# Layer 0 of a four-layer convolution network: the statistics of image 0 on partitions of (channel, half of the image)

## The chip, the cores and the metric

The kernel runs on one core of a Trainium2 chip. The metric is the device time in microseconds of one execution; lower is better. A core has a matrix engine (TensorE, PE in the profile), a vector engine (VectorE, DVE), an activation engine (ScalarE, ACT), GpSimd (POOL), a sync engine (SyncE, SP) that in this kernel issues the loads, and 16 DMA engines that move data between HBM and the on-chip memory. That memory has 128 partitions.

## The reference

The input `x` has 4 images of 64 channels of 256 x 256, in float32. Four layers follow one another, each a residual around a convolution of a group norm:

```python
def _gn(v, G=32, eps=1e-5):
    B_, C_, H_, W_ = v.shape
    g = v.reshape(B_, G, C_ // G, H_, W_)
    m = jnp.mean(g, axis=(2, 3, 4), keepdims=True)
    s = jnp.var(g, axis=(2, 3, 4), keepdims=True)
    return ((g - m) / jnp.sqrt(s + eps)).reshape(v.shape)

x = x + _L0_conv_ref(_gn(x), w_in, w_dw, fft_filter, w_out)
x = x + _L1_conv_ref(_gn(x), kernel)
x = x + _L2_conv_ref(_gn(x), core, periphery, threshold, scale, 1, 1)
x = x + _L3_conv_ref(_gn(x), weights1, weights2)
```

The group norm takes mean and variance of 2 neighbouring channels over the whole image, so nothing of layer 0 can be normalized for an image before all of that image has been read once. Layer 0 then expands 64 channels to 384, multiplies 8 x 8 patches by a filter in the frequency domain, applies a 3 x 3 depthwise convolution, gates one half of the channels by the gelu of the other, and projects back to 64. Layer 1 is a 3 x 3 convolution, layer 2 a choice between two convolutions by a local difference measure, layer 3 a multiplication of low Fourier modes.

## The kernel before, in words

The four layers run one after the other, each from HBM to HBM. Layer 0 has two phases.

*The statistics of image 0* (L256 to L263) come first and alone. A loop over NJ = 32 steps allocates a tile `st` of 128 partitions x 4 rows x 256 columns out of 12 buffers and fills it with two loads (L261), which SyncE issues: channels of one band of four rows into partitions 0 to 63, channels of the next band into partitions 64 to 127. So a partition is (band of the pair, channel), each load moves 64 rows of 4 KB, and within a load the rows are a whole channel, 256 KiB, apart. VectorE runs two `bn_stats` of 512 columns on each tile (L253, in `input_stats`), which leave count, mean and squared deviation of each piece per partition.

`group_norm_parts` (L153 to L175) makes scale and bias of them: `bn_aggr` to mean and variance per partition (`mv`, L158), a TensorE product with the 128 x 128 matrix `avg` that averages the means over a group of partitions (L161), a copy of the result (`gm`, L163), the deviation of each partition from it (`d`, L165) and its square plus the variance (`q`, L167), a second product with `avg` (L170), then the power -0.5 on GpSimd (`r`, L174) and `nb` = -mean · r on VectorE (L175). `avg` joins the partitions of the same group, which are (half, channel) in everything that comes after: `r` and `nb` are read by `normalize` as scale and bias of partitions (half of the columns, channel).

After that SyncE loads the constants of the layer (`c_fdft` to `woutc`, L138, L279, L283 and L286), into memory that the `st` buffers held, and then the first tiles of `x` (L306). ScalarE normalizes a tile (L210), TensorE transposes and transforms it (L346, L356), and the main loop begins: 128 steps, each with one tile of 8 rows through all parts of the layer. In the loop the order of instructions on TensorE, VectorE, ScalarE and SyncE is the order in which they are written. The statistics of the other images are taken inside this loop, one tile a step (`load_stats`, L568, and `next_stats`), while TensorE is busy; they have the old partition layout and are not touched by the change.

Of the statistics phase, the order is set by the queues: SyncE issues the loads in order and waits with each until the load eight before it has landed, and from the thirteenth tile on until `bn_stats` has freed the buffer; VectorE waits for the load of its tile.

Of the kernel before, what the change touches and what calls it, by code (L numbers as in the profile page):

```python
# [17 lines left out]
C = 64  # L18
# [3 lines left out]
GROUPS = 32  # L22
# [4 lines left out]
def _patch_dft():  # L27


    p = PATCH  # L30
    h, w = np.meshgrid(np.arange(p), np.arange(p), indexing="ij")
    rows, pick = [], []
    for kw in range(p // 2 + 1):
        edge = kw in (0, p // 2)
        for kh in range(p // 2 + 1 if edge else p):
            ang = 2 * np.pi * (kh * h + kw * w) / p
            sel = np.zeros((p, p // 2 + 1))
            sel[kh, kw] += 0.5 if edge else 1.0
            if edge:
                sel[(-kh) % p, kw] += 0.5  # L40
            rows.append(np.cos(ang).ravel())
            pick.append(sel.ravel())
            if not (edge and kh in (0, p // 2)):
                rows.append(np.sin(ang).ravel())
                pick.append(sel.ravel())
    fwd = np.array(rows)
    inv = np.linalg.inv(fwd)
    pick = np.array(pick)
    twice = lambda m: np.concatenate([m, m], 0)
    return twice(fwd.T), twice(inv.T), twice(pick).T  # L50


def _fno_dft(H, W):
    m = MODES
    kh = np.concatenate([np.arange(m), np.arange(-m, 0)])
    kw = np.arange(m)
    ah = 2 * np.pi * np.outer(np.arange(H), kh) / H
    eh = np.stack([np.cos(ah), -np.sin(ah)], -1).reshape(128, H // 128, 4 * m)
    aw = 2 * np.pi * np.outer(np.arange(W), kw) / W
    cw, sw = np.cos(aw), np.sin(aw)  # L60
    ew = np.stack([np.concatenate([cw, -sw], 1), np.concatenate([sw, cw], 1)], 1)
    ew = ew.reshape(W // 128, 128, 2, 2 * m)
    ei = np.stack([np.cos(ah), -np.sin(ah)], 0).transpose(2, 0, 1)
    ei = ei.reshape(2, m, 2, H).transpose(2, 1, 0, 3).reshape(2 * m, 2, H)
    ck = np.where(kw == 0, 1.0, 2.0)[:, None] / (H * W)
    iw = np.concatenate([ck * cw.T, -ck * sw.T], 0)
    return eh, ew, ei, np.concatenate([iw] * 4, 0)


def _constants(H, W):  # L70
    f_blk, b_blk, pick = _patch_dft()
    eh, ew, ei, iw = _fno_dft(H, W)
    grp = (np.arange(128) % C) // (C // GROUPS)
    avg = (grp[:, None] == grp[None, :]) / np.sum(grp == 0)
    half = np.arange(128) // C
    ones = half[:, None] == half[None, :]


    g32 = (np.arange(128) % 32) // (C // GROUPS)
    avg32 = (g32[:, None] == g32[None, :]) / np.sum(g32 == 0)  # L80
    chan = np.arange(128) % C
    sel32 = np.stack([np.arange(128)[:, None] + 32 * k == chan[None, :] for k in range(2)], 1)
    sel32[32:] = False
    out = {
        "c_ident": np.eye(128), "c_avg32": avg32, "c_sel32": sel32, "c_fdft": f_blk, "c_bdft": b_blk, "c_pick": pick, "c_avg": avg,
        "c_ones": ones, "c_eh": eh, "c_ew": ew, "c_ei": ei, "c_iw": iw,
    }
    return {k: np.ascontiguousarray(v, dtype=np.float32) for k, v in out.items()}
# [26 lines left out]
class _Net:  # L115
# [34 lines left out]
        for _ in self.group_norm_parts(*args):  # L150
            pass

    def group_norm_parts(self, n, b, bst, psum):  # L153


        nc, sp = self.nc, self.sp
        mv = sp.tile([128, 2], F32, tag="mv", name=f"mv{n}_{b}")
        nc.vector.bn_aggr(mv, bst.rearrange("p n s -> p (n s)"))  # L158
        yield
        ps = psum(f"gn{n}_{b}")  # L160
        nc.tensor.matmul(ps[:, 0:1], self.avg, mv[:, 0:1], start=True, stop=True)  # L161
        gm = sp.tile([128, 1], F32, tag="gm", name=f"gm{n}_{b}")
        nc.vector.tensor_copy(gm, ps[:, 0:1])  # L163
        d = sp.tile([128, 1], F32, tag="gd", name=f"gd{n}_{b}")
        nc.vector.tensor_sub(d, mv[:, 0:1], gm)  # L165
        q = sp.tile([128, 1], F32, tag="gq", name=f"gq{n}_{b}")
        nc.vector.scalar_tensor_tensor(q, d, d, mv[:, 1:2], ALU.mult, ALU.add)  # L167
        yield
        ps2 = psum(f"gv{n}_{b}")
        nc.tensor.matmul(ps2[:, 0:1], self.avg, q, start=True, stop=True)  # L170
        v = sp.tile([128, 1], F32, tag="gv", name=f"gvs{n}_{b}")
        nc.vector.tensor_scalar(v, ps2[:, 0:1], EPS, None, ALU.add)
        r, nb = self.r[n][:, b : b + 1], self.nb[n][:, b : b + 1]
        nc.gpsimd.tensor_tensor(r, v, self.mhalf, ALU.pow)  # L174
        nc.vector.scalar_tensor_tensor(nb, gm, -1.0, r, ALU.mult, ALU.mult)  # L175
# [53 lines left out]
    def _layer0(self, ctx, dst):  # L229
        tc, nc, a, B, H, W = self.tc, self.nc, self.a, self.B, self.H, self.W  # L230
# [4 lines left out]
        def pair(name):  # L235

            return pp.tile([128, 2, 512], F32, tag=f"p{next(turn) % 4}", name=name)

        small = lambda name: pair(name)[:, 0, :]
# [4 lines left out]
        halves = [slice(0, C), slice(C, 128)]  # L244
        quarters = [slice(k * Q, (k + 1) * Q) for k in range(4)]

        src_t = a["x"].rearrange("b c (j s r) w -> b c j s r w", r=4, s=2)

        def input_stats(t, k, bst):
            tf = t.rearrange("p r w -> p (r w)")  # L250
            n = 4 * W // 512
            for i in range(n):
                nc.vector.bn_stats(bst[:, k * n + i, :], tf[:, i * 512 : (i + 1) * 512])  # L253

        new_bst0 = lambda b: self.stats_tile(f"bst0_{b}", NJ * 4 * W // 512)
        with tc.tile_pool(name="l0i", bufs=12) as p_i:  # L256
            bst0 = new_bst0(0)
            for k in range(NJ):
                t = p_i.tile([128, 4, W], F32, tag="st", name=f"st_{k}")
                for s in range(2):  # L260
                    nc.sync.dma_start(t[halves[s]], src_t[0, :, k, s])  # L261
                input_stats(t, k, bst0)
            self.group_norm(0, 0, bst0, small)  # L263

        cp = pool("l0c", 1)
        p_st, p_x, p_r, p_xn = pool("l0st", 2), pool("l0x", 2), pool("l0r", 2), pool("l0xn", 1)
# [3 lines left out]
        pick, filt = self.load("c_pick", cp), self.load("filt", cp)  # L270
        wdw = self.load("w_dw", cp)
        ps = small("psf")
# [1095 lines left out]
```

## Time and profile before

The time before is 7649.04 us, the median of 3 runs from 7638.49 to 7653.11. The profiled execution has a span of 7652.4 us.

| engine | busy us | share of the span |
|---|---|---|
| PE, matmul | 7291.6 | 95% |
| PE, weight load | 4324.6 | 57% |
| DVE | 6594.1 | 86% |
| ACT | 3656.9 | 48% |
| POOL | 637.7 | 8% |

The busy shares are averages over the whole span. The table by stretches is of more use for a change in one place; the first five stretches, of 20 us each, show how the kernel begins. The last column is what the DMA engines moved.

| stretch, us | PE busy | DVE busy | ACT busy | GB/s |
|---|---|---|---|---|
| 0 to 20 | 0.00 | 8.17 | 0.00 | 211 |
| 20 to 40 | 0.00 | 11.79 | 0.00 | 239 |
| 40 to 60 | 0.00 | 11.40 | 0.00 | 239 |
| 60 to 80 | 1.84 | 12.73 | 0.00 | 176 |
| 80 to 100 | 6.83 | 3.37 | 6.53 | 88 |

The first load of `st` is issued at 1.67 us, the last at 66.0 us; a load takes between 3.4 and 9.2 us from its issue to its landing, 8.7 us in the middle. The last `bn_stats` ends at 75.48 us. ScalarE runs its first normalize at 88.47 us.

### The profile page before, as it was taken

The numbers are of one execution on the slowest core, as the hardware profiler recorded it, in microseconds if no ns is written. First come the engines' busy times: TensorE is split into PE (matmuls) and PEld (weight loads), VectorE is DVE, ScalarE is ACT, GpSimd is POOL, SyncE is SP. The second block draws the span as 40 slices with busy tenths as digits, with TensorE's granted clock in tenths as the row PEclk, the third lists the DMA queues.
The fourth block names the chain that finished last, engine by engine and source line by source line (L and its number), as shares of the span: only waits on it lengthen the run. The fifth ranks groups of instructions, "written<-read, shape, count | busy, mean of one in ns | idle before, by whom it ended". The sixth has DMA issues, their size and how long they took to land.

```text
span 7652.4 us, 398676 instructions
## 1 busy us (share of the span) xinstructions
PE 7291.6 (95%) x189302; PEld 4324.6 (57%) x189302; DVE 6594.1 (86%) x5914; ACT 3656.9 (48%) x3917; POOL 637.7 (8%) x1403
## 2 busy tenths in 40 slices
PE   5999999999999999999999999899989999997887
PEld 3666666666666666666666666433334444443375
DVE  6999999999999999999999999899979989884345
ACT  2445444445454444544444454322238787773111
POOL 0000000000000000000000000010102222221000
PEclk9999999999999999999999999999999999999955
DMA  5222222222222222222111211477766666666689
GB/s 119 62 66 63 59 62 60 59 62 60 64 59 59 60 62 60 65 59 53 45 47 47 49 47 44 113 196 196 198 150 178 176 172 179 172 175 236 226 325 390
DMA packets 502418, 875.49 MB, mean 114 GB/s; under 512 B 42948, under 2 KB 306068, under 8 KB 483380
## 3 DMA queue, kind: packets, MB, share of 16 engines
q1 hardware_dynamic: 420276, 581.48, 27.7%
q0 software_dynamic: 80512, 268.50, 12.2%
q8 instruction: 1485, 24.33, 1.4%
q14 instruction: 145, 1.19, 0.0%
HBM read 581.37 MB, written 268.44 MB: 111 GB/s over the span
## 4 chain that ended last, share of the span: by engine, by line
PE 88%; DVE 4%; DMA 4%; issue 2%; ACT 1%; SPq 0%; DVEq 0%; ACTq 0%; POOLq 0%; POOL 0%
PE psd L434 31%; PE psy L407 10%; PE m L786 9%; PE psu L369 9%; PE one L1038 7%; PE div L997 5%; PE pso L509 3%; DMA x<-x 3%; DVE v L472 2%; PE psz L1027 2%; PE psa L1212 2%; PE psF L356 2%; PE psT L346 2%; PE m L794 1%; PE pso L500 1%
## 5 line engine op out<-in xcount | busy, mean ns | idle before, releaser
L434 PE MATMUL psd<-y,diag 32*32 32x512 f32 x73296 | 2536.7, 597 | 7.5 <-issue 6.1
L472 DVE SCALAR_TENSOR_TENSOR v<-y,sb_w_dw,v 128x2048 f32<-128x2048 f32 x1024 | 2390.8, 2335 | 109.8 <-ACT v L470 87.1
L434 PEld LDWEIGHTS psd<-y,diag 32*32 32x32 f32 x73296 | 1526.1, 103 | 852.5 <-issue 333.8
L414 ACT COPY y<-psy 128x512 f32<-128x512 f32 x1536 | 915.6, 660 | 1691.0 <-PE psy L407 1689.0
L372 DVE TENSOR_TENSOR up<-psu,flt 128x768 f32<-128x768 f32 x1024 | 932.6, 951 | 223.4 <-PE psu L369 222.5
L407 PEld LDWEIGHTS psy<-sb_c_bdft,up 64*64 64x64 f32 x49152 | 858.4, 135 | 345.3 <-issue 132.2
L407 PE MATMUL psy<-sb_c_bdft,up 64*64 64x64 f32 x49152 | 930.2, 221 | 27.5 <-issue 24.6
L369 PE MATMUL psu<-win,xf 64*64 64x384 f32 x8192 | 788.2, 487 | 19.8 <-DVE h L454 10.0
L983 DVE TENSOR_TENSOR q<-xn 128x2313 f32<-128x2313 f32 (+2 forms) x256 | 627.3, 2494 | 10.4 <-ACT xn L210 10.4
L1038 PE MATMUL one<-z,wp 32*32 32x512 f32 x16384 | 591.5, 596 | 17.1 <-issue 14.0
L984 ACT ACTIVATE q<-q 128x2313 f32<-128x2313 f32 (+2 forms) x256 | 529.0, 2086 | 31.2 <-DVE q L983 29.7
L210 ACT ACTIVATE xn<-x,nb,r 128x1024 f32<-128x1024 f32 (+3 forms) x272 | 488.1, 1798 | 57.7 <-DMA x<-x 54.0
L448 ACT ACTIVATE h<-psd 128x1024 f32<-128x1024 f32 x258 | 251.0, 1023 | 516.9 <-PE psd L434 516.7
L1038 PEld LDWEIGHTS one<-z,wp 32*32 32x32 f32 x16384 | 369.9, 103 | 219.8 <-issue 77.9
L997 PE MATMUL div<-q,ones 64*32 64x512 f32 x8192 | 465.1, 596 | 10.3 <-ACT q L984 9.3
L369 PEld LDWEIGHTS psu<-win,xf 64*64 64x64 f32 x8192 | 306.1, 134 | 185.1 <-issue 84.9
L379 POOL MEMSET y<- 128x22 f32 x384 | 51.7, 136 | 4238.0 <-ACT y L387 3175.2
L1071 POOL DMA_DIRECT2D x<-r x512 | 272.8, 540 | 977.2 <-DVE r L1068 949.4
L786 PE MATMUL m<-t,wg 64*64 64x512 f32 x3072 | 343.4, 591 | 11.0 <-DVE t L779 11.0
L786 PE MATMUL m<-t,wk 64*64 64x512 f32 x3072 | 352.7, 588 | 0.0
L997 PEld LDWEIGHTS div<-q,ones 64*32 64x32 f32 x8192 | 153.0, 107 | 314.9 <-issue 243.4
L801 ACT COPY s<-m 128x1024 f32<-128x1024 f32 x64 | 64.8, 1013 | 542.5 <-PE m L786 542.5
(131 smaller groups left out, 7616.3 us busy)
## 6 DMA issues: line engine op xcount, KB each, us to landing
x<-x SPq DMA_DIRECT2D x240, 640.0 KB, 5.7
x<-x SPq DMA_DIRECT2D x61, 2048.0 KB, 12.6
st<-in_x_dram SPq DMA_DIRECT2D x256, 256.0 KB, 3.6
x<-in_x_dram SPq DMA_DIRECT2D x256, 256.0 KB, 3.8
x<-o POOLq DMA_DIRECT2D x128, 512.0 KB, 8.5
r<-x SPq DMA_DIRECT2D x512, 128.0 KB, 4.0
x<-r POOLq DMA_DIRECT2D x512, 128.0 KB, 3.9
out_dram<-x POOLq DMA_DIRECT2D x32, 2048.0 KB, 13.3
```

Source lines behind the costliest of these rows:

```text
L210: self.nc.scalar.activation(dst, src, AF.Identity, bias=self.nb[n][p0:p1, b : b + 1], scale=self.r[n][p0:p1, b : b + 1])
L369: nc.tensor.matmul(ps[halves[n], s, 0:384], xf[t][halves[s], n, 4 * g + k], win[halves[s]], start=True, stop=True)
L372: nc.vector.tensor_mul(ups[t, g][:, :, k, :], ps[:, :, 0:384], flt.broadcast_to([128, 2, 384]))
L407: nc.tensor.matmul(ps[halves[c], n, s, :, k, :], up[halves[n], s, k, i * 128 + c * C : i * 128 + (c + 1) * C], bdft[halves[n]], start=True ...
L414: nc.scalar.copy(yt[t][i][:, 3:11, w0 : w0 + 64].rearrange("p r (k n w) -> p n r k w", k=4, n=2), ps[:, :, s])
L434: ins = nc.tensor.matmul(d[q // 2][quarters[j], q % 2], diag[quarters[q], i, k, :], rows_in(t, i, quarters[q], j, dy)[:, :, dx : dx + W], ...
L472: nc.vector.scalar_tensor_tensor(v, s, wdw[:, 2, k : k + 1], v, ALU.mult, ALU.add)
L786: nc.tensor.matmul(rows2(m)[halves[j], s], gs[i][halves[s], dx, :], ts[n][halves[s], i, 2 * j : 2 * j + 2, dx : dx + W], start=(dx == 0), ...
L983: nc.vector.tensor_sub(d, p0, p1)
L984: nc.scalar.activation(d, d, AF.Square)
L997: ins = nc.tensor.matmul(ps[quarters[j], h], ones[halves[h]], q[n, g, k][halves[h], r + 2 * j : r + 2 * j + 2, o : o + W], start=(m == 0), ...
L1038: ins = nc.tensor.matmul(rows2(ps[g])[quarters[j], k], w[quarters[i]], z[quarters[i], h, 2 * j + dy : 2 * j + dy + 2, dx : dx + W], tile_p ...
```

## The change

The statistics of image 0 are taken on partitions of (channel, half of the image): partition 2c + s holds the rows of half s of channel c. In HBM that is a plain view of the image as 128 rows, each 128 KiB after the one before, so one load fills all 128 partitions of a `st` tile, and the 64 loads of 256 KB become 32 of 512 KB. The tile, its 12 buffers and the two `bn_stats` on it stay.

The group norm then finds its per-partition numbers in another layout than its results are needed in. Two more constant matrices serve that. `c_avgp` averages groups within the new layout and gives each partition the mean that its deviation is measured from. `c_avgx` averages groups of the new layout and writes the result in the old one, (half, channel), so that `r` and `nb` come out where `normalize` reads them. It is used for the mean a second time (one more matmul, and one more copy, into the same tile `gm`) and for the second product. Both matrices are loaded from a pool of their own, `l0a`, ahead of the `st` tiles. The group norms of the other images and layers pass no such pair and run as before.

```diff
+    grpp = np.arange(128) // 2 // (C // GROUPS)
+    avgp = (grpp[:, None] == grpp[None, :]) / np.sum(grp == 0)
+    avgx = (grpp[:, None] == grp[None, :]) / np.sum(grp == 0)
...
-    def group_norm_parts(self, n, b, bst, psum):
+    def group_norm_parts(self, n, b, bst, psum, avg=None):
+        same, moved = avg or (self.avg, self.avg)
...
-        nc.tensor.matmul(ps[:, 0:1], self.avg, mv[:, 0:1], start=True, stop=True)
+        nc.tensor.matmul(ps[:, 0:1], same, mv[:, 0:1], start=True, stop=True)
+        if moved is not same:
+            nc.tensor.matmul(ps[:, 1:2], moved, mv[:, 0:1], start=True, stop=True)
         gm = sp.tile([128, 1], F32, tag="gm", name=f"gm{n}_{b}")
         nc.vector.tensor_copy(gm, ps[:, 0:1])
...
         nc.vector.scalar_tensor_tensor(q, d, d, mv[:, 1:2], ALU.mult, ALU.add)
+        if moved is not same:
+            nc.vector.tensor_copy(gm, ps[:, 1:2])
         yield
         ps2 = psum(f"gv{n}_{b}")
-        nc.tensor.matmul(ps2[:, 0:1], self.avg, q, start=True, stop=True)
+        nc.tensor.matmul(ps2[:, 0:1], moved, q, start=True, stop=True)
...
-        with tc.tile_pool(name="l0i", bufs=12) as p_i:
+        with tc.tile_pool(name="l0i", bufs=12) as p_i, tc.tile_pool(name="l0a", bufs=1) as p_a:
             bst0 = new_bst0(0)
+            flat = a["x"][0].rearrange("c (s h) w -> (c s) (h w)", s=2)
+            avgs = [self.load(name, p_a) for name in ("c_avgp", "c_avgx")]
             for k in range(NJ):
                 t = p_i.tile([128, 4, W], F32, tag="st", name=f"st_{k}")
-                for s in range(2):
-                    nc.sync.dma_start(t[halves[s]], src_t[0, :, k, s])
+                nc.sync.dma_start(t.rearrange("p r w -> p (r w)"), flat[:, 4 * W * k : 4 * W * (k + 1)])
                 input_stats(t, k, bst0)
-            self.group_norm(0, 0, bst0, small)
+            self.group_norm(0, 0, bst0, small, avgs)
```

More of the change, by code (lines that the diff above doesn't have):

```diff
@@ L84, in _constants @@
     out = {
-        "c_ident": np.eye(128), "c_avg32": avg32, "c_sel32": sel32, "c_fdft": f_blk, "c_bdft": b_blk, "c_pick": pick, "c_avg": avg,
+        "c_ident": np.eye(128), "c_avg32": avg32, "c_sel32": sel32, "c_fdft": f_blk, "c_bdft": b_blk, "c_pick": pick, "c_avg": avg, "c_avgp": avgp, "c_avgx": avgx,
         "c_ones": ones, "c_eh": eh, "c_ew": ew, "c_ei": ei, "c_iw": iw,
```

## The prediction

> **What bounds the kernel now.** I read the page first: TensorE is busy 95% of 7652.4 us and the chain that ended last lies 88% on it, so for most of the span a DMA change would buy nothing. The page's slices also show TensorE at 5 tenths in the first slice, and that is where the change is. So the second view is the chain of waits from 0 to 100 us, whose columns are start, length and what the time was spent on:
>
> ```profile
> 6.11 6.81 DMA st<-in_x_dram
> 12.94 8.77 DMA st<-in_x_dram
> ...
> 65.98 8.11 DMA st<-in_x_dram
> 74.19 1.30 DVE bst L253 x2
> ...
> 82.60 4.52 DMA x<-in_x_dram
> 87.18 1.28 ACT L210
> 88.47 1.25 ACT xn L210
> ```
>
> From 6 to 74 us nothing but the loads of `st` is on the path. Then come the last two bn_stats, constants, and loads of `x`; the first normalize starts at 88.47. Third, the timeline of VectorE at the two ends of this stage, and the group of instructions of L253 in the first 110 us (count, busy us, mean ns, idle before them):
>
> ```profile
> 6.44 1.29 DVE L253 BATCH_NORM_STATS2 bst<-st 128x6 f32<-128x512 f32 x2 [5.57 <-DMA st<-in_x_dram]
> ...
> 74.19 1.29 DVE L253 BATCH_NORM_STATS2 bst<-st 128x6 f32<-128x512 f32 x2 [0.46 <-DMA st<-in_x_dram]
> ```
>
> ```profile
> L253 DVE BATCH_NORM_STATS2 bst<-st 128x6 f32<-128x512 f32 x64 | 41.2, 685 | 33.4 <-DMA st<-in_x_dram 33.4
> ```
>
> Each tile has 1.29 us of statistics and then a wait. 31 tile periods fill 74.19 - 6.44 = 67.75 us, 2.185 us each; 524,288 bytes in 2.185 us are 240 GB/s. Fourth, the engines by stretch; the last two numbers of each line are the DMA engines' busy share and GB/s:
>
> ```profile
> 10.00:30.00 20.00, 0.00 (x0) 0.00 (x0) 11.57 (x18) 0.00 (x0) 0.00 (x0) 1.00 1.04 238
> ...
> 7400.00:7500.00 100.00, 82.88 (x463) 63.50 (x463) 59.09 (x95) 12.41 (x21) 8.18 (x10) 0.59 1.04 408
> ```
>
> ```profile
> 7279.00:7282.00 3.00, 3.00 (x62) 3.00 (x61) 0.00 (x0) 0.00 (x0) 0.00 (x0) 0.50 1.02 437
> ```
>
> All three have the DMA engines fully busy, at very different rates. 238 GB/s is the 64-partition `st` loads; 408 is layer 3, with loads and stores on 128 partitions; 437 is a pure load of `wt` on 128 partitions. So the first stage is bound by slow transfers, not by too few of them or by their issue.
>
> **What the Trainium skill says.** First, "SBUF — State Buffer", section "Door 1: The DMA port swizzle": partitions 0 to 63 and 64 to 127 each reach only 8 of the 16 ports, for a ceiling of about 218 GB/s against 436. Its next section, "Can I just issue two DMAs to hit both halves?", answers no (6% gained). The trace agrees in kind: pairs of half transfers make 240 GB/s, somewhat over that ceiling, and 128-partition ones 408 to 437. Second, "DMA: Bandwidth & Descriptors", section "iDMA fabric — 4 AXI ports for 8 engines, asymmetric across TPBs", has a load stream from SP with rows of 4 KiB at 408.7 GB/s, a figure it calls unchecked; its transfers are of 1 MiB, ours will be of 512 KB with the same rows. Third, the same page, "Latency and other measured facts", warns that a row pitch of large powers of two (512 KiB and more) can slow a copy. After the change the pitch is 128 KiB. The trace speaks against harm there: a row of `wf` is 2·16·1024 floats, 128 KiB as well, and `wt` came at 437 GB/s, though in runs of 16 KiB.
>
> **The change, part by part.**
>
> *Transfers.* 64 half transfers of 256 KB become 32 of 512 KB on all partitions. Bytes and 4 KB rows are the same. Period of a tile at full speed: at 408 GB/s, 524,288/408,000 = 1.285 us; at 437, 1.20; at 322 GB/s, which the 2 KB-row loads of layer 3 made between 7020 and 7056 us with TensorE reading beside them, 1.63. I take 1.285: rows of 4 KB lie between the 2 KB of the 322 GB/s loads and the 16 KB of `wt`, and it is also the figure of the skill.
>
> *VectorE.* The same 64 bn_stats. Where four of 512 columns run together (L826) they take 2.47 us, the last of them 0.68, so one starts every (2.47 - 0.68)/3 = 0.60 us and a tile costs 1.19 us. That is below 1.285, so VectorE nearly becomes the bound but does not; at 437 GB/s the two tie.
>
> *Issue.* A `st` issue starts every 0.64 us in the first eight, below 1.285, so SyncE stays ahead. Up to eight loads are in flight (an issue waits for the eighth before it), now 4 MB, about 10 us of data, well over the latency. The twelve buffers are freed by bn_stats as before.
>
> *Two more constants.* Issues of `ident` and `avg` are 0.46 us apart, so the first `st` goes out at 1.67 + 0.92 = 2.59 us. In the kernel before, from first issue to first bn_stats were 6.44 - 1.67 = 4.77 us; less a tile's 2.185 that is 2.59 us of latency. The first bn_stats comes at 2.59 + 2.59 + 1.285 = 6.46 us: the smaller first tile pays for the constants.
>
> *Sum of the stage.* Last pair at 6.46 + 31·1.285 = 46.3, end at 47.6 us, against 75.48 before: 27.9 us less.
>
> *Group norm.* One more matmul (two passes; the present L161 takes 0.59 us) and one more copy of 128x1 (0.16 us). The copy of the second mean has no wait of its own in the changed program's order, so the first copy probably waits for both matmuls: up to 0.6 us later for `gm`, `gd`, `gq`; the new copy then lies under the matmul L170 (0.68 us of VectorE's idle time). Queued behind on VectorE are `diag` and `flt`, finished at 83.84 us before, and behind on TensorE the matmul L273. Who waits for them: `r` and `nb`, ready at 80.38 us, are needed by the normalize at 88.47, which waited for `x` until 87.1. The whole chain can slip by over 6 us for nothing, so I count 0.
>
> *The SyncE queue after the stage.* It issues `fdft` at 75.50, right after the last bn_stats, and needs 6.4 us of constants before the first `x`. In the changed program that first load waits, as before, for all `st` loads and VectorE. The new constants are read by TensorE until some 4 us later, but no load waits for TensorE before those of `r`, long after. So this piece moves forward whole.
>
> *The rest.* Order and waits of everything from the first normalize on are unchanged, and nothing there is tied to absolute time. The stage is serial, so 27.9 us come off the end: 7649.0 - 27.9 = 7621.
>
> **Rivals.**
>
> *A, forecast: 128-partition loads at 400 to 437 GB/s.* 7621, and 7619 if VectorE binds at about 1.20. For it: the DMA share of 1.04 at both 238 and 408 GB/s.
>
> *B, a half gain: HBM rows of 4 KB limit it to about 322 GB/s.* First pair at 2.59 + 2.59 + 1.63 = 6.8, end at 6.8 + 50.5 + 1.3 = 58.6 us, 17 us less: 7632. For it: isolated layer 3 loads made no more. Against: these have 2 KB rows and gaps between them.
>
> *C, no gain: the limit is the source, not the partitions.* Period 2.185 stays, the two constants add 0.9 us: 7650. Against: `wt` with the same pitch.
>
> *D, slower: the 128 rows at a power-of-two pitch get in one another's way more than the 64 at 256 KiB.* Taking the fall the skill gives for 2 MiB against a padded pitch (164 to 214 GB/s) as an estimate, 240 becomes 184 GB/s, 2.85 us a tile, end at 8.0 + 88.4 + 1.3 = 97.7 us: 22 us more, 7671. Against: the same `wt` line.
>
> **How the numbers follow.** A 0.79, B 0.12, C 0.06, D 0.03. The three times of before lie within 14.6 us, so a median may be 7 us off. 0.2% is 15.3 us: faster means below 7633.7. A always is, B somewhat more often than not, so faster 0.86, same 0.11, slower 0.03. The range takes A with VectorE as bound, less noise and a little for another chip (7608), up to B with its noise (7640); C and D and the tails, some 0.15, are outside.
>
> **What would show it.** The `st` stretch at 400 GB/s or more; the last bn_stats ending near 47.6 us; VectorE's waits for `st` in this stage falling from 33.4 us to about 6.5 at the start and then some 0.1 us a tile; 32 issues of 512 KB; the first normalize near 60.6 us, still waiting for `x`. I am wrong if the GB/s stays near 240 (C), lands near 320 (B), if `fdft` goes out later than the last bn_stats, or if the normalize waits for `nb` and not for `x`.

## The result, and the profile after

The changed kernel takes 7623.63 us, the median of 6 runs, beside 7646.99 us for 6 runs of the kernel before; the ratio is 0.9969, 95% interval [0.9956, 0.9982]. The forecast was 7621. In the profiled executions the spans are 7652.4 us before and 7624.4 after.

First the chain of waits of the changed kernel from 0 to 75 us (start, length, what the time was spent on):

```profile
3.08 5.49 DMA st<-in_x_dram
8.59 1.29 DVE bst L263 x2
9.90 1.29 DVE bst L263 x2
11.20 37.09 DVE bst L263 x58
...
55.47 4.41 DMA x<-in_x_dram
60.09 1.28 ACT L220
61.39 1.25 ACT xn L220
```

The long row of `DMA st` pieces is gone. From the second tile on the chain runs over VectorE's statistics until 48.29 us; before, the last of them ended at 75.48. That VectorE sets the pace does not follow from this: the chain goes back to the instruction before on the same engine where the record of that instruction reaches up to the next start, and here it does. What the statistics wait for is settled below, by starts and landings. Behind that the picture is the old one: constants, loads of `x`, table load, normalize. The first normalize moved from 88.47 to 61.39 us, 27.1 us, and the end of the statistics 27.2.

The group of the statistics in the first 110 us (count, busy us, mean ns, idle before), and then the engines by stretch, whose last two numbers are the DMA engines' busy share and GB/s:

```profile
L263 DVE BATCH_NORM_STATS2 bst<-st 128x6 f32<-128x512 f32 x64 | 40.9, 685 | 6.5 <-DMA st<-in_x_dram 6.4
```

```profile
10.00:20.00 10.00, 0.00 (x0) 0.00 (x0) 9.98 (x16) 0.00 (x0) 0.00 (x0) 1.00 1.03 412
20.00:30.00 10.00, 0.00 (x0) 0.00 (x0) 10.00 (x17) 0.00 (x0) 0.00 (x0) 1.00 1.03 410
```

VectorE's waits fell from 33.4 to 6.5 us, nearly all of it for the first two tiles (5.5 and 0.9). The DMA engines are as busy as before (1.03) and move 410 GB/s where they moved 238. VectorE looks busy for the whole of each stretch too; whether it or the loads set the pace is the question of a run below.

### The profile page after: what moved, and what is told of

It reads as the page before. It is cut to its first block, busy times and chain, and to the rows that moved or that the text cites. A ratio compares the mean times of both kernels' runs of the same rounds, so it can differ in the third digit from the quotient of the medians.

```text
span 7624.4 us, 398618 instructions
## 1 busy us (share of the span) xinstructions
PE 7287.0 (96%) x189304; PEld 4324.9 (57%) x189304; DVE 6593.1 (86%) x5915; ACT 3657.8 (48%) x3917; POOL 638.0 (8%) x1403
## 4 chain that ended last, share of the span: by engine, by line
PE 88%; DVE 5%; DMA 4%; issue 2%; ACT 1%; SPq 0%; POOL 0%; DVEq 0%; POOLq 0%; ACTq 0%
PE psd L446 31%; PE psy L419 10%; PE m L798 9%; PE psu L381 9%; PE one L1050 7%; PE div L1009 6%; DMA x<-x 3%; PE pso L521 3%; DVE v L484 2%; PE psz L1039 2%; PE psa L1224 2%; PE psF L368 2%; PE psT L358 2%; PE m L806 1%; PE pso L512 1%
## 5 line engine op out<-in xcount | busy, mean ns | idle before, releaser
L1009 PE MATMUL div<-q,ones 64*32 64x512 f32 x8192 | 465.5, 596 | 10.2 <-ACT q L996 10.1
## 6 DMA issues: line engine op xcount, KB each, us to landing
out_dram<-x POOLq DMA_DIRECT2D x32, 2048.0 KB, 13.1
```

The source lines that it names most:

```text
L1009: ins = nc.tensor.matmul(ps[quarters[j], h], ones[halves[h]], q[n, g, k][halves[h], r + 2 * j : r + 2 * j + 2, o : o + W], start=(m == 0), ...
```

## The experiments

Each set of runs shares the runs of the kernel before on its own chip, whose median was 7625 or 7650 us, or a single run of 7658, by set; times are only compared within a set, and readings of the first stage come from the traces.

**Is it the partitions of one transfer, or the source?** The new layout stays, the tile is filled in halves again:

```diff
-                nc.sync.dma_start(t.rearrange("p r w -> p (r w)"), flat[:, 4 * W * k : 4 * W * (k + 1)])
+                for s in range(2):
+                    nc.sync.dma_start(
+                        t[halves[s]].rearrange("p r w -> p (r w)"), flat[halves[s], 4 * W * k : 4 * W * (k + 1)]
+                    )
```

> The new layout and group norm stay, but each tile is filled again by two loads of 64 partitions. My theory, that the span of partitions of one transfer sets the rate: a tile every 2.18 us as in the kernel before, about 240 GB/s, the last bn_stats ends near 76 us and the time is that of before plus up to 1 us for the two constants, near 7648. Rival, that the source (rows at a pitch of 128 KiB, a contiguous image) is what made the loads fast: about 410 GB/s and an end near 48 us, time near 7624.

The engines by stretch of this kernel:

```profile
20.00:30.00 10.00, 0.00 (x0) 0.00 (x0) 5.30 (x9) 0.00 (x0) 0.00 (x0) 1.00 1.04 233
```

It makes 233 to 235 GB/s, and the last `bn_stats` ends at 78.15 us, 2 us later than expected. The time is that of before: 7623.43 beside 7625.42 us, ratio 0.9997 [0.9988, 1.0005]. With the layout, the group norm and the constants of the change, but without whole loads, nothing is gained. The source is not the cause.

**Do the halves only have to be in flight together?** In the kernel before, loads of the lower and the upper half already take turns in one queue. Here they come from two; the edit is shown against the kernel with halves:

```diff
-                    nc.sync.dma_start(
+                    (nc.sync, nc.scalar)[s].dma_start(
                         t[halves[s]].rearrange("p r w -> p (r w)"), flat[halves[s], 4 * W * k : 4 * W * (k + 1)]
                     )
```

> As the halves, but the upper half of each tile is issued by ScalarE, the lower by SyncE, so that loads of both halves are in the DMA engines at once. If only a single transfer over all partitions uses the whole width: near 240 to 255 GB/s, end of the statistics near 72 to 76 us, time near 7645. Rival, that it was the strict turn of lower and upper halves in one queue that held the loads back: 350 to 410 GB/s, end near 48 to 55 us, time near 7625 to 7632.

```profile
20.00:30.00 10.00, 0.00 (x0) 0.00 (x0) 6.33 (x10) 0.00 (x0) 0.00 (x0) 1.00 1.04 243
```

It makes 237 to 244 GB/s, ends at 75.85 us and takes 7623.62 us, ratio 0.9999 [0.9990, 1.0007]. A second queue gives a few per cent of rate here, and no time; the Trainium skill ("SBUF — State Buffer", section "Can I just issue two DMAs to hit both halves?") has 6% for two concurrent transfers over a single one.

**Or the size of a load?** The whole loads were also the larger ones (512 against 256 KB), so the two runs above leave that open. Two kernels separate it. One has tiles of 8 rows, filled by two loads of 64 partitions of 512 KB each:

> In the runs so far the loads of 64 partitions were also the loads of 256 KB. Here tiles of 8 rows are filled by two loads of 64 partitions with rows of 8 KB: 512 KB a load, as in the changed kernel. If the span of partitions sets the rate: about 240 GB/s, 4.4 us a tile, last bn_stats near 77 us. Rival, that the size of a load sets it: about 410 GB/s, end near 49 us.

The other has tiles of 4 rows, filled by two loads over 128 partitions of 256 KB each:

```diff
+                for s in range(2):
+                    at = (4 * k + 2 * s) * W
+                    nc.sync.dma_start(t[:, 2 * s : 2 * s + 2].rearrange("p r w -> p (r w)"), flat[:, at : at + 2 * W])
```

> The other way round: each tile of 4 rows is filled by two loads over all 128 partitions of 2 rows each, so 64 loads of 256 KB with rows of 2 KB. If the span of partitions sets the rate: 380 to 410 GB/s (the shorter rows may cost some), end at 48 to 51 us. Rival, that the size of a load sets it: near 240 GB/s, end near 76 us.

The same view of the two, the one with large halves first:

```profile
20.00:30.00 10.00, 0.00 (x0) 0.00 (x0) 5.51 (x10) 0.00 (x0) 0.00 (x0) 1.00 1.02 221
```

```profile
20.00:30.00 10.00, 0.00 (x0) 0.00 (x0) 10.00 (x15) 0.00 (x0) 0.00 (x0) 1.00 1.05 387
```

Large halves make 222 GB/s and end at 83.36 us, 6 us later than expected; small whole loads make 383 to 392 and end at 50.40. So it is not the size of a load, and not the bytes in flight either: with eight loads in flight the small whole loads have 2 MB there, as the kernel before. What is left is that a load spans 128 partitions and not 64. Whether the number of partitions counts, that of the rows a load takes to them, or which partitions it reaches, no run here separates. Halves of 512 KB are even a little slower than those of 256 KB, and come close to the ceiling of about 218 GB/s that the Trainium skill ("SBUF — State Buffer", section "Door 1: The DMA port swizzle") gives for 64 partitions; that smaller pieces in turn get above it because the two halves then overlap more is a guess. Each of the two ran once, 7675.43 and 7631.12 us beside 7657.56 us for the kernel before.

**Was the new layout needed for that?** Old layout and old group norm, one load a tile, with the band as outermost dimension of the source:

```diff
-                for s in range(2):
-                    nc.sync.dma_start(t[halves[s]], src_t[0, :, k, s])
+                nc.sync.dma_start(t.rearrange("p r w -> p (r w)"), src_t[0, :, k].rearrange("c s r w -> s c (r w)"))
```

> The kernel before, its old layout (band, channel) and old group norm kept, but each tile loaded by one transfer: the source has three dimensions (2 bands, 64 channels, 1024), the tile two (128, 1024). Rival to the need for the new layout: any single transfer over 128 partitions runs at 410 GB/s, end near 48 us, time near 7620. My theory, from the Trainium skill (DMA: Bandwidth & Descriptors, section on why a DMA increments its semaphore by 16), which says that the number of DMA engines must divide the outermost dimension of both sides: 2 engines, some 52 GB/s by 2/16 of 410, 10 us a tile, end near 330 us, time near 7900.

The engines by stretch, and the last statistics in the timeline of VectorE:

```profile
20.00:30.00 10.00, 0.00 (x0) 0.00 (x0) 1.29 (x2) 0.00 (x0) 0.00 (x0) 1.00 0.13 52
```

```profile
319.66 1.29 DVE L253 BATCH_NORM_STATS2 bst<-st 128x6 f32<-128x512 f32 x2 [8.88 <-DMA st<-in_x_dram]
329.81 1.28 DVE L253 BATCH_NORM_STATS2 bst<-st 128x6 f32<-128x512 f32 x2 [8.86 <-DMA st<-in_x_dram]
```

The DMA share of 0.13 is 2/16, so two engines work, as the rule in the Trainium skill ("DMA: Bandwidth & Descriptors", section "Why a DMA increments its semaphore by 16 and not by 1") gives for outermost dimensions of 2 and 128. The rate of 52 GB/s, 10.2 us a tile and the end at 331.1 us agree with the estimate made from it; the one run took 7877.62 us. Whole loads are wanted, but of a source that has 128 as its own outermost dimension; that is what the layout of (channel, half) buys.

**What bounds the stage now?** One `bn_stats` a tile (half of image 0 left out of its statistics):

```diff
-            bst0 = new_bst0(0)
+            bst0 = self.stats_tile("bst0h_0", NJ)
...
-                input_stats(t, k, bst0)
+                nc.vector.bn_stats(bst0[:, k, :], t.rearrange("p r w -> p (r w)")[:, 0:512])
```

> The changed kernel with one bn_stats a tile in place of two: the statistics of image 0 leave out half of the image. VectorE then needs 0.68 us a tile. If the loads bind at 410 GB/s (1.28 us a tile): waits of about 0.6 us before each tile, last bn_stats ends near 47.6 us against 48.3. Rival, that VectorE had become the bound at 1.28 us a tile and the loads can do more: 437 GB/s, 1.20 us a tile, end near 44.5 us.

VectorE's timeline of this kernel:

```profile
45.36 0.69 DVE L274 BATCH_NORM_STATS2 bst0h<-st 128x6 f32<-128x512 f32 x1 [0.59 <-DMA st<-in_x_dram]
46.61 0.69 DVE L274 BATCH_NORM_STATS2 bst0h<-st 128x6 f32<-128x512 f32 x1 [0.55 <-DMA st<-in_x_dram]
```

With half the work on VectorE waits of 0.6 us come back, the loads stay at 411 GB/s and a tile at 1.28 us, and the end moves by 1.0 us only, to 47.30, of which 0.6 is the missing second half of the last tile. (The one run took 7594.94 us beside 7625.42.) So the loads set the pace of the changed kernel, and do not become faster when VectorE has less to do. Its SyncE queue agrees: 23 issues of `st` waited for the load eight before, none for a buffer that VectorE had to free.

```profile
SPq L273 <- DMA st<-in_x_dram: 20.9, 23, 1.2
```

Do VectorE and the loads tie? A pair of `bn_stats` fills 1.28 us in the timeline of the changed kernel, as long as a load. But the record of a `bn_stats`, 0.68 us, is longer than the time after which the next can start. In the kernel with two queues two tiles sometimes are there together, and then four `bn_stats` follow one another, the third with the load of its own tile to wait for:

```profile
42.80 2.47 DVE L263 BATCH_NORM_STATS2 bst<-st 128x6 f32<-128x512 f32 x4 [1.77 <-DMA st<-in_x_dram]
```

They start 0.59 to 0.61 us apart, from one tile to the next as within a tile, so a tile costs VectorE 1.20 us. In the changed kernel the first `bn_stats` of a tile starts 0.67 us (0.63 to 0.69) after the last of the tile before, and 0.02 us after its own load has landed, in all of the 24 tiles whose landing can be read from the trace. So VectorE still waits some 0.07 us for each tile. The view shows no gap, because the record of the `bn_stats` before reaches over it. VectorE comes close to the loads, with 6% in hand.

Then the other side, tiles of 8 rows, with four `bn_stats` behind each wait:

> The changed kernel with 16 tiles of 8 rows (1 MB a load, 6 buffers) in place of 32 of 4 rows, so that four bn_stats stand behind each wait. If a wait costs VectorE the overlap with the bn_stats before it: 2.48 us a tile of 8 rows in place of 2 x 1.28, below the 2.56 us of its load at 410 GB/s, so waits of about 0.1 us a tile come back; the first tile lands 1.3 us later, and the last one has 1.2 us more to do: end near 48.6 us, no gain. Rival, that larger loads run faster (430 GB/s and above): waits stay small, 2.44 us a tile, end near 47 us.

Neither end of it was quite right. In the timeline of VectorE, with the idle time before each row in brackets:

```profile
7.65 29.91 DVE L263 BATCH_NORM_STATS2 bst<-st 128x6 f32<-128x512 f32 x48 [6.78 <-DMA st<-in_x_dram]
38.35 9.88 DVE L263 BATCH_NORM_STATS2 bst<-st 128x6 f32<-128x512 f32 x16 [0.78 <-DMA st<-in_x_dram]
```

Loads of 1 MB make 419 to 425 GB/s, and 48 `bn_stats` take 29.91 us, 2.49 us a tile of 8 rows, less than 2 x 1.28. That is again the time of a load: 1,048,576 bytes in 2.49 us are 421 GB/s, and each tile's first `bn_stats` starts 0.02 us after its landing (12 tiles of 16 can be read). So the larger loads with their rows of 8 KB are a little faster; that a wait costs VectorE its overlap, as was expected here, is not so. The later first tile, the longer last one and one load that came 0.8 us late take the gain back: the end is at 48.23 us (one run, 7631.59 us beside 7650.11). The kernel with small whole loads, where every `bn_stats` has a load to wait for, agrees: 61 of them take 41.23 us, 0.68 each, and those whose landing can be read (48 of 64) start within 0.05 us of it; 262,144 bytes in 0.676 us are 388 GB/s, the rate of the loads.

**Is the group norm hidden, and what is still in the way?** Between the last statistics and the first normalize stay 13.1 us, filled by the issue of constants and the loads of `x`. Constants, win, wout and the first two tiles of `x` get memory of their own and are loaded behind the `st` tiles:

```diff
+        cp, p_x = pool("l0c", 1), pool("l0x", 2)
...
                 input_stats(t, k, bst0)
+            early = {}
+            for t in range(2):
+                early[t] = p_x.tile([128, 8, HW2], F32, tag="x", name=f"x0_{t}")
+                for s in range(2):
+                    nc.sync.dma_start(early[t][halves[s]], a["x"][0, :, 8 * t : 8 * t + 8, s * HW2 : (s + 1) * HW2])
+            fdft, bdft = self.load("c_fdft", cp), self.load("c_bdft", cp)
...
             self.group_norm(0, 0, bst0, small, avgs)
```

> The changed kernel with the constants of layer 0 and the first two tiles of x in memory of their own, loaded right behind the st tiles rather than after the last bn_stats. If the first normalize waits for x alone and the group norm of the image is hidden: it moves from 61.4 us to the arrival of nb, near 54.0 us, and the time falls by a further 7.4 us, a ratio near 0.9955 to before. Rival, that the group norm chain or the table load then takes longer than it looks (VectorE works on diag between its steps): normalize at 56 us or later, 5 us or less.

> As the one with constants and x early, and the two new constants c_avgp and c_avgx are loaded behind the st tiles, not ahead of them. If their issue ahead of the first st is what they cost: the whole stage moves 0.9 us forward, last bn_stats at 47.4 us, normalize near 53.1 us. Rival, that the loads' latency hides it: 48.3 us as before.

For comparison the changed kernel ran once more in the same set:

> The changed kernel itself once more, beside the others of this set. If the shorter first stage is all there is: 27 us less than before on the same chip, a ratio near 0.9964, its last bn_stats at 48.3 us and first normalize at 61.4 us. Rival, that part of the gain is given back later (the first measurement had 23 us): a ratio of 0.9970 or above again.

| kernel | last statistics end | first normalize | second normalize | time | ratio to before |
|---|---|---|---|---|---|
| changed, again | 48.06 | 61.29 | 68.61 | 7632.71 | 0.9971 [0.9960, 0.9983] |
| constants and `x` early | 49.61 | 54.97 | 64.25 | 7622.70 | 0.9965 [0.9951, 0.9979] |
| and the two new constants late | 48.14 | 53.49 | 61.22 | 7614.70 | 0.9957 [0.9945, 0.9970] |

The lines of the last one in order of time, `nb` being the end of the group norm:

```profile
46.85 1.29 DVE L263 BATCH_NORM_STATS2 bst<-st 128x6 f32<-128x512 f32 x2 [1.03 <-DMA st<-in_x_dram]
...
50.30 1.28 ACT L220 ACT_TABLE_LOAD   x1 [50.30 <-DMA x<-in_x_dram]
...
53.30 0.16 DVE L185 SCALAR_TENSOR_TENSOR nb<-gm,r 128x1 f32<-128x1 f32 x1 [0.69 <-POOL r L184]
53.49 1.24 ACT L220 ACTIVATE xn<-x,nb,r 128x1024 f32<-128x1024 f32 x1 [1.92 <-DVE nb L185]
```

Now the normalize waits for `nb`, so in the changed kernel the group norm was hidden behind the loads of `x`. Loading early brings the first normalize 6.3 us forward, about 1 us less than expected, since the last statistics ended 1.5 us later than in the kernel run beside it. The second gains only 4.4: the product of `filt` and `c_pick` (L301, 1.6 us on the path) now falls between the two, in the middle of the first tile's transform, where before it was done while `x` was waited for. With `c_avgp` and `c_avgx` late the first `bn_stats` starts at 5.58 us and not at 6.45, and the second normalize is 7.4 us earlier than in the changed kernel. The last statistics do not gain from that: the last `st` tile, now with the small rows of `x` behind it, came late (1.03 us of waiting in the line above); that the rows of `x` delay it was not tested. This version beats both kernels by its median; the intervals of the ratios overlap with the changed kernel's, so that it is faster rests on the traces' 7.4 us more than on the times.

The changed kernel's second ratio, 0.9971, is again a little above the 0.9964 of the stage alone. From the first normalize to the issue of layer 1's weights (L723, L735) its first profile took 4785.2 us, the kernel before 4789.0; on another chip the kernel with halves took 4760.9 us there and the one with half the statistics 4763.5. No steady give-back is to be seen in that, but differences of 3 to 4 us are what these traces cannot tell. Whether a few of the 27 us are lost later stays open; 27 lies inside both intervals.

## Why the prediction was right

*The bound.* The loads of `st` were the whole path, and their rate was the lever: the runs with halves show it. They are the path of the changed kernel still: its statistics start with the landings.

*The period of a tile.* 1.285 us at 408 GB/s was taken; the loads make 408 to 412, 1.28 us. The reasoning that 4 KB rows lie between the two measured cases held; the loads with 2 KB rows made 387 rather than the 322 GB/s that rival B leaned on, so the low rate of those loads of layer 3 is not due to their rows alone. That 408 fits so closely is in part luck: in the trace it stood for loads and stores together, and the figure of the skill for transfers of 1 MiB, which here, with rows of 8 KB, made 419 to 425.

*VectorE.* The 1.19 us a tile, taken from four `bn_stats` in a row, holds across tiles with a wait each: 1.20 us in the kernel with two queues. So VectorE nearly binds and does not, as forecast, and waits some 0.07 us a tile, where 0.1 were forecast. A busy share of 100% and the chain of waits say otherwise only because they count the whole record of a `bn_stats`.

*The first tiles.* The first `bn_stats` was forecast at 6.46 us and came at 6.38; the second tile came 2.2 us after it and not 1.285, which is more than the difference between the forecast end, 47.6 us, and 48.29. The forecast gave every tile after the first the full rate, and why the second falls short of it was not tested. In the second profile of the same kernel it was 1.8 us.

*Group norm.* The mean's copy did wait for both matmuls: from the end of the statistics to `nb` it takes 5.3 us after and 4.9 before. The forecast allowed up to 0.6 and counted 0, since the normalize waits for `x`; moving `x` forward showed that.

*The queue after the stage.* `fdft` goes out at 48.30 us, right behind the last statistics; nothing waits for the new constants' memory.

*The sum.* 27.9 us forecast, 27.1 at the first normalize, 28.0 in the spans; the medians differ by 23.4 us, by 17.4 in the set with the second run, and the ratios stand for 22 to 24 us, with intervals some 10 us either way. So it is the traces of the stage that bear the sum out; the times agree with it, and with a few us less. Rival C, no gain by the source, is what the halves showed to be false; D, a loss by the pitch of the rows, likewise, since the same pitch gives 410 GB/s.

## What to carry to other kernels

Where a stage waits for loads and the DMA engines are fully busy, compare their GB/s with a stretch of the same trace that loads all 128 partitions: at an equal busy share, 238 against 408, as here, means that the transfers and not their number are the matter. Arrange the source so that its outermost dimension is the 128 partitions, and pay for the other layout where it is cheap, here in two small matrices and two tiny instructions. Ask which of two close limits binds by starts and landings, not by busy shares: an engine that starts each piece as its load lands is waiting, even when its records leave no gap. When that stage is done, look at what stands between it and the next: loads that wait for its buffers can often have memory of their own.

## What the runs showed of the hardware

A `bn_stats` of 512 columns starts 0.59 to 0.61 us after another if its data are there, within a tile and from one tile to the next (four over two tiles in 2.47 us), while its own record lasts about 0.68 us. One load over 128 partitions whose source has 2 as its outermost dimension ran at 52 GB/s, an eighth of 410. Loads of 256 KB over 128 partitions, eight in flight, made 387 GB/s, so size mattered little here beside the span: 387, 410 and about 420 GB/s for 256 KB, 512 KB and 1 MB, where the first also had rows half as long as the second.
